# The last stage of a fused transformer kernel put in source order on all compute engines, with the sums of the generated weights moved from GpSimd to VectorE

## The chip, the cores and the metric

The kernel runs on one core of one Trainium2 chip. The metric is the device time of one launch in microseconds, the median of the runs. Lower is better. The engines have short names in the profile: PE is TensorE (PEld its weight loads), DVE is VectorE, ACT is ScalarE, POOL is GpSimd, and SP is SyncE, which here only issues DMAs.

## The reference, cut to what matters

Input `x` has 64 sequences of 64 tokens with 256 features; `cond_256` has a vector of 64 numbers for each sequence. Four layers follow each other, all in float32:

```
x = x + quantised_gelu_ffn(rmsnorm(x) * (cond @ norm_w.T + 1))             # L0
x = x + alpha_a * attention(gamma_a * rmsnorm(x) + beta_a)                 # L1, 16 heads of 16
x = x + alpha_f * (silu(n @ gate_w.T) * (n @ hidden_w.T) @ out_w.T + out_b)
                              # n = gamma_f * rmsnorm(x) + beta_f, 256 -> 1024 -> 256
x = (layernorm(x) * w + b + tanh(cond @ lin_w.T + lin_b)) * w + b          # L2
Wd_b = Wd + 0.1 * (cond @ Wdd.T + bdd)                                     # L3: weights of its own
Wu_b = Wu + 0.1 * (cond @ Wdu.T + bdu)                                     #     for every sequence
x = x + relu(x @ Wd_b.T + bd) @ Wu_b.T + bu                                #     256 -> 128 -> 256
```

## The kernel before

The 4096 tokens are cut into 8 blocks of 512 tokens (`NBLK` = 8, 8 sequences each). Three stages follow each other: L0 (to about 290 us of the profile), attention (to about 470 us), and a last stage with the gated feed-forward layer of L1, the layer norm L2 and the adapter L3. The change is in the last stage and in its opening.

The last stage loops over `n` from 0 to 63; `i, f = divmod(n, 8)` gives the block `i` and the tile `f` of 128 of the 1024 hidden features. The steps of one `n` are:

- `f_products(n)`: 12 matmuls of 512 columns into two banks `gh` (the gate and the hidden value; each float32 product is made of three matmuls of split numbers in `mm3`, lines 83 to 85). There are four `gh` banks.
- `f_inner(n)`: ACT takes silu of the gate (line 622), DVE multiplies it with the value into `sg` (line 623).
- `f_parts(n, sg)`: ACT rounds `sg` to `hhi` (line 642), DVE makes the rest `hlo` (line 643).
- `f_outer(n)`: 12 matmuls of 256 columns that add this tile's share to the two `acc` banks. It is called two steps late, as `f_outer(n - 2)`.

Beside these run, for the block before, its end: `f_residual` (DVE: times alpha, line 667; plus `x2`, line 670; the layer norm's statistics, lines 672 and 673; POOL: the inverse root, lines 182 and 184; DVE: subtract the mean and scale, line 676, called the centring below), `f_weights` (SP loads the generated weights `wd` and `wu` of the block; POOL adds their common part `bias` to them, line 692, four adds of 128x1024 for each block), `f_adapt` (four PE transposes of `x3` and a DVE operation, lines 702 and 703, once for each half `c`), `f_down` and `f_up` (64 small matmuls each, lines 713 and 727). For the block after, `f_start` loads and scales `x2` (lines 191 and 205), and `f_norm` turns it and splits it (lines 212 to 216, 198 and 199). `f_rows` loads two sets of rows, `alpha` and `ab`, and POOL adds `ab` to `x2` (line 606, two adds of 128x512). `f_last` does the end of block 7.

Two ways of ordering are used. Inside `tc.manual_schedule(engines=...)` PE, ACT, DVE and POOL issue in the order of the source; outside it a planner orders each engine's queue by its own costs. Before, the region under manual order opens with attention and closes after `f_outer(3)`, ahead of the loop from `n = 5`. SP is not among its engines: the planner orders the DMAs throughout, and issues a load as soon as its buffer is free. Buffers are counted by tag: `ab` and `alpha` have one each, `wd` and `wu` four, `mm` two banks in this stage.

## Time and profile before

| | |
|---|---|
| median of 3 runs | 807.06 us (805.04 to 807.66) |
| the profiled execution: its own time / span | 804.37 us / 802.2 us |
| PE busy | 763.5 us (95% of the span) |
| DVE, ACT, POOL busy | 567.2, 370.5, 325.7 us |
| PE clock granted, mean | 0.985 |
| chain that ended last | PE 79%, DVE 9%, issue 4%, POOL 3%, DMA 3% |

The page comes from one execution. "Busy" is the time in which an engine works on an instruction. A row of the view by windows gives, for a stretch of time, the busy time of each engine with the number of instructions in parentheses, then the granted PE clock (1.00 is full), the DMA share and GB/s. A row of the timeline gives start, duration, engine, source line, operation, output and inputs with their shapes; a bracket at its end gives the idle time of the engine before it and what ended that.

### The profile page before, as it was taken

How to read it: one execution, taken by the hardware profiler on the slowest of the kernel's cores; microseconds unless marked ns; L12 is line 12 of the kernel's file. 1: busy time of each engine (PE TensorE's matmuls, PEld its weight loads, DVE VectorE, ACT ScalarE, POOL GpSimd, SP SyncE). 2: the span in 40 equal slices, each digit the busy share in tenths (PEclk: the TensorE clock that was granted, in tenths of full speed). 3: DMA queues.
4: the chain of work that ended last, by engine and by line, in shares of the span. 5: the costliest groups of instructions: out<-in, count | busy, mean ns of one | idle time of the engine just before them, and what ended most of it. 6: DMA issues, size and time to landing. Idle time of an engine off the chain costs nothing.

```text
span 802.2 us, 17323 instructions
## 1 busy us (share of the span) xinstructions
PE 763.5 (95%) x7014; PEld 620.2 (77%) x7014; DVE 567.2 (71%) x935; ACT 370.5 (46%) x758; POOL 325.7 (41%) x300
## 2 busy tenths in 40 slices
PE   5999999999999979999999999879999999999996
PEld 3676766667667868888887878778888888888885
DVE  4885866667667679999989875555666666665755
ACT  6524542443443558887877673223233333333130
POOL 2212221222225315545545316945454545454500
PEclk9989999999999999999999999989999999999999
DMA  8997989878884764545655129616161616160401
GB/s 296 308 252 223 233 230 241 203 221 206 190 259 106 145 158 96 131 133 133 153 139 120 40 69 236 131 28 180 35 180 39 173 44 167 50 161 28 133 1 54
DMA packets 117135, 118.87 MB, mean 148 GB/s; under 512 B 39568, under 2 KB 100624, under 8 KB 117056
## 3 DMA queue, kind: packets, MB, share of 16 engines
q1 hardware_dynamic: 109568, 92.40, 46.1%
q0 software_dynamic: 7488, 25.37, 10.4%
q8 instruction: 55, 0.90, 0.5%
q14 instruction: 24, 0.20, 0.1%
HBM read 71.41 MB, written 29.56 MB: 126 GB/s over the span
## 4 chain that ended last, share of the span: by engine, by line
PE 79%; DVE 9%; issue 4%; POOL 3%; DMA 3%; ACT 1%; SPq 0%; DVEq 0%; POOLq 0%; ACTq 0%
PE mm L83 10%; PE mm L84 10%; PE mm L85 10%; PE gh L83 7%; PE gh L85 6%; PE gh L84 6%; PE mm L251 4%; PE acc L85 4%; PE mm L363 4%; PE acc L84 4%; PE acc L83 4%; DMA x2d<-ax 2%; PE mm L520 2%; PE mm L212 2%; PE mm L713 2%
## 5 line engine op out<-in xcount | busy, mean ns | idle before, releaser
L83 PE MATMUL mm<-up,xhl 128*128 128x512 f32 x256 | 108.9, 425 | 2.2 <-ACT up L280 2.2
L84 PE MATMUL mm<-up,xhl 128*128 128x512 f32 x256 | 102.8, 402 | 0.1
L85 PE MATMUL mm<-up,xll 128*128 128x512 f32 x256 | 102.5, 401 | 0.0
L83 PE MATMUL gh<-xhf,gh 128*128 128x512 f32 x244 | 99.2, 407 | 0.0
L84 PE MATMUL gh<-xlf,gh 128*128 128x512 f32 x244 | 95.6, 392 | 0.5 <-POOL xlf L199 0.5
L85 PE MATMUL gh<-xhf,gh 128*128 128x512 f32 x244 | 95.8, 393 | 0.0
L642 ACT CAST hhi<-sg 128x512 fp32r<-128x512 f32 x61 | 37.9, 621 | 119.1 <-DVE sg L623 119.1
L337 DVE SCALAR_TENSOR_TENSOR h<-mm,rs_l,g 128x512 f32<-128x512 f32 x64 | 47.7, 745 | 59.5 <-PE mm L85 36.5
L623 DVE TENSOR_TENSOR sg<-gh,sg 128x512 f32<-128x512 f32 x61 | 41.7, 683 | 64.8 <-PE gh L85 58.2
L85 PE MATMUL acc<-wout,hlo 128*128 128x256 f32 x256 | 74.0, 289 | 7.9 <-DVE hlo L643 7.9
L83 PEld LDWEIGHTS mm<-up,xhl 128*128 128x128 f32 x256 | 49.2, 192 | 38.5 <-issue 18.7
L336 ACT ACTIVATE g<-mm,rs_l 128x512 f32<-128x512 f32 x64 | 44.0, 687 | 73.0 <-PE mm L85 66.9
L83 PE MATMUL acc<-wout,hhi 128*128 128x256 f32 x256 | 73.4, 287 | 1.6 <-ACT hhi L642 1.6
L643 DVE TENSOR_TENSOR hlo<-sg,hhi 128x512 fp32r<-128x512 f32 x61 | 54.6, 895 | 26.7 <-ACT hhi L642 26.3
L84 PE MATMUL acc<-wout,hhi 128*128 128x256 f32 x256 | 73.3, 286 | 0.0
L216 POOL TENSOR_TENSOR xg<-xg,cv 128x512 f32<-128x512 f32 x32 | 33.2, 1046 | 70.7 <-DVE xg L215 70.7
L622 ACT ACTIVATE sg<-gh 128x512 f32<-128x512 f32 x61 | 36.3, 595 | 50.6 <-PE gh L85 50.6
L261 ACT COPY stg<-mm 128x512 f32<-128x512 f32 x64 | 35.3, 587 | 50.9 <-PE mm L251 50.9
L85 PEld LDWEIGHTS mm<-up,xll 128*128 128x128 f32 x256 | 49.0, 192 | 11.9
L84 PEld LDWEIGHTS mm<-up,xhl 128*128 128x128 f32 x256 | 49.3, 193 | 9.8 <-DVE up L281 0.6
L85 PEld LDWEIGHTS acc<-wout,hlo 128*128 128x128 f32 x256 | 49.5, 193 | 8.6 <-DVE hlo L643 8.6
L85 PEld LDWEIGHTS gh<-xhf,gh 128*128 128x128 f32 x244 | 46.0, 188 | 10.7
(189 smaller groups left out, 1905.7 us busy)
## 6 DMA issues: line engine op xcount, KB each, us to landing
gt<-in_g SPq DMA_DIRECT2D x32, 512.0 KB, 4.7
rows<-alphad SPq DMA_DIRECT2D x48, 256.0 KB, 4.0
s1d<-stg POOLq DMA_DIRECT2D x32, 256.0 KB, 5.1
s2d<-stg POOLq DMA_DIRECT2D x32, 256.0 KB, 4.8
vb<-vx SPq DMA_DIRECT2D x32, 256.0 KB, 4.5
wd<-s1d SPq DMA_DIRECT2D x32, 256.0 KB, 4.5
wu<-s2d SPq DMA_DIRECT2D x32, 256.0 KB, 5.6
xf<-in_xT SPq DMA_DIRECT2D x8, 512.0 KB, 7.0
```

What stands on the lines that cost most here:

```text
L83: nc.tensor.matmul(out, lhsT=l[0], rhs=r[0], start=first, stop=False)
L84: nc.tensor.matmul(out, lhsT=l[0], rhs=r[1], start=False, stop=False)
L85: nc.tensor.matmul(out, lhsT=l[1], rhs=r[0], start=False, stop=last)
L216: nc.gpsimd.tensor_tensor(b3(xg), b3(xg), bc(vb, c, i), ALU.add)
L251: nc.tensor.matmul(pb[s][c * 64:(c + 1) * 64], lhsT=gl[h], rhs=gt[h, c * GC:(c + 1) * GC], start=True, stop=True, tile_position=(64 * s, 6 ...
L261: nc.scalar.copy(stg[:, s], pb[s])
L336: nc.scalar.activation(g, pg, AF.Gelu, scale=rs[:, t:t + 1])
L337: nc.vector.scalar_tensor_tensor(h[:, ch * 512:(ch + 1) * 512], pv, rs[:, t:t + 1], g, ALU.mult, ALU.mult)
L622: nc.scalar.activation(sg, pg, AF.Silu)
L623: nc.vector.tensor_tensor(sg, pv, sg, ALU.mult)
L642: nc.scalar.copy(h_hi, sg)
L643: nc.vector.tensor_tensor(h_lo, sg, h_hi.bitcast(F32), ALU.subtract)
```

## The change

1. The manual order now holds to the end of the kernel, so the loop from `n = 5` and `f_last` are issued in source order on PE, ACT, DVE and POOL.
2. The four adds of `bias` go from POOL to DVE (`f_common`) and are spread over the steps `f` = 0, 0, 3 and 6 of the next block.
3. `f_residual` is cut into `f_residual` (`f` = 1), `f_stats` (`f` = 2) and `f_center` (`f` = 3). `f_rows` only loads; the POOL adds of `ab` are `f_base`, called at `f` = 3 of the block's own steps. `f_start` is cut into its load, squares and scaling at `f` = 2, 3 and 4.
4. In the opening, the silu of the three kept tiles is a step of its own (`f_silu`), the first of them inside the last step of attention; `f_inner(4)` and `a_project` change places with products.
5. In the end, the products of tiles 62 and 63 are done for one half of the tokens first, the up products of block 6 come behind them, and `f_last`'s steps are taken by halves. The down products of block 6 go into the loop.

```
 in attention's last step:   todo.append((lambda: None) if tp == 0 else (lambda: f_silu(0)))
...
     s3 = f_inner(3)
     a_weigh(W - 1)
+    f_silu(2)
     s2 = f_kept(2)
     a_parts(W - 1)
     f_outer(0)
+    s4 = f_inner(4)
+    f_parts(2, s2)
     f_outer(1)
-    f_parts(2, s2)
     f_parts(3, s3)
-    a_project(W - 1)
     f_rows(0)
+    f_base(0)
     f_start(1)
-    s4 = f_inner(4)
+    a_project(W - 1)
     f_outer(2)
     f_parts(4, s4)
     f_outer(3)
-    ordered.close()
...
+    for n in range(5, N):
+        i, f = divmod(n, 8)
+        for rest in late:
+            rest()
+        late = []
+        sg = f_inner(n)
+        if i > 0 and f in (4, 5):
+            f_adapt(i - 1, f - 4)
+        if i + 1 < NBLK and f in (5, 6):
+            late = [norm_turn(*fblk[i + 1]["n"], i + 1, f - 5, V_FG, V_FB)]
+        if i > 0 and f == 6:
+            f_down(i - 1)
+        if 0 < i < NBLK - 1 and f == 7:
+            pus = f_up_products(i - 1)
+        f_parts(n, sg)
+        if n > 5:
+            f_outer(n - 2)
+        if 0 < i < NBLK - 1 and f == 7:
+            f_up_store(i - 1, pus)
...
+        if i > 0:
+            if f == 0:
+                f_common(i - 1, "wd", 0)
+                f_common(i - 1, "wd", 1)
+            if f == 1:
+                f_residual(i - 1)
+            if f == 2:
+                f_stats(i - 1)
+            if f == 3:
+                f_center(i - 1)
+                f_base(i)
+                f_common(i - 1, "wu", 0)
+            if f == 6:
+                f_common(i - 1, "wu", 1)
+        if f == 2 and i > 0:
+            f_rows(i)
+            if i + 1 < NBLK:
+                f_load(i + 1)
+        if f == 3 and i + 1 < NBLK and i > 0:
+            f_begin(i + 1)
+        if f == 4 and i + 1 < NBLK and i > 0:
+            f_scale(i + 1)
+        if f == (6 if i + 1 < NBLK else 1):
+            f_weights(i)
...
+    f_last(NBLK - 1)
+    ordered.close()
```

The new helpers, whose bodies were part of `f_rows`, `f_residual` and `f_weights`:

```
+    def f_base(i):
+        x2, ab = fblk[i]["x2"], fblk[i]["ab"]
         for tp in range(TT // 2):
             s = slice(2 * tp, 2 * tp + 2)
             nc.gpsimd.tensor_tensor(x2[:, s], x2[:, s], ab[:, s], ALU.add)
...
+    def f_center(i):
+        B = fblk[i]
+        x3, mv, rs = B["x3"], B["mv"], B["rln"]
         for t in range(TT):
             nc.vector.tensor_scalar(x3[:, t], x3[:, t], mv[:, t, 0:1], rs[:, t:t + 1], ALU.subtract, ALU.mult)
...
+    def f_common(i, which, k):
+        w = fblk[i][which][k]
...
+        nc.vector.tensor_tensor(w, w, row.unsqueeze(1).broadcast_to([P, 4, D]), ALU.add)
```

In `f_last`, the order of the first steps:

```
+        for k in range(2):
+            for n in (8 * i + 6, 8 * i + 7):
+                f_outer(n, range(2 * k, 2 * k + 2))
+        pus = f_up_products(i - 1)
...
+        scaled(0)
+        added(0)
...
+        f_up_store(i - 1, pus)
```

More of the change, by code (lines that the diff above doesn't have):

```diff
@@ L601, in f_rows @@
         fblk[i]["at"] = load_rows(1, "alpha", i)
-        ab = load_rows(2, "ab", i)
-        x2 = fblk[i]["x2"]
+        fblk[i]["ab"] = load_rows(2, "ab", i)
+    def f_base(i):
+        x2, ab = fblk[i]["x2"], fblk[i]["ab"]
         for tp in range(TT // 2):
@@ L630, in f_keep, with f_silu @@
         nc.vector.tensor_copy(room[n][:, 1], pv)
+    def f_silu(n):
+        nc.scalar.activation(room[n][:, 0], room[n][:, 0], AF.Silu)
     def f_kept(n):
         g, v = room[n][:, 0], room[n][:, 1]
-        nc.scalar.activation(g, g, AF.Silu)
         nc.vector.tensor_tensor(g, v, g, ALU.mult)
@@ L644, in f_parts, with f_outer @@
         fun[n] = (h_hi, h_lo)
-    def f_outer(n):
+    def f_outer(n, tiles=range(TT)):
         i, f = divmod(n, 8)
-        h_hi, h_lo = fun.pop(n)
+        h_hi, h_lo = fun[n]
         wout = pools["wout"]
-        if f == 0:
+        if f == 0 and "acc" not in fblk[i]:
             fblk[i]["acc"] = [bank("acc") for _ in range(2)]
         acc = fblk[i]["acc"]
-        for t in range(TT):
+        for t in tiles:
             ts = slice(t * P, (t + 1) * P)
@@ L658, in f_residual, with f_stats @@
     def f_residual(i):
+        B = fblk[i]
+        x3 = B["x3"] = block(f"x3_{i}")
+        for tp in range(TT // 2):
+            s = slice(2 * tp, 2 * tp + 2)
+            nc.vector.tensor_tensor(x3[:, s], B["acc"][tp].rearrange("p (t d) -> p t d", d=D), B["at"][:, s], ALU.mult)
+    def f_stats(i):
         pool = pools["c"]
         B = fblk[i]
-        x2, at = B["x2"], B["at"]
-        x3 = block(f"x3_{i}")
+        x2, x3 = B["x2"], B["x3"]
         st = pool.tile([P, TT, 6], F32, tag="bst", bufs=2, name=f"bst{i}")
-        mv = pool.tile([P, TT, 2], F32, tag="bmv", bufs=2, name=f"bmv{i}")
-        for tp in range(TT // 2):
-            s = slice(2 * tp, 2 * tp + 2)
-            nc.vector.tensor_tensor(x3[:, s], B["acc"][tp].rearrange("p (t d) -> p t d", d=D), at[:, s], ALU.mult)
+        mv = B["mv"] = pool.tile([P, TT, 2], F32, tag="bmv", bufs=2, name=f"bmv{i}")
         for tp in range(TT // 2):
@@ L673, in f_residual @@
                 nc.vector.bn_aggr(mv[:, t], st[:, t])
-        rs = rsqrt(mv[:, :, 1], 1.0, 1e-5, f"ln{i}")
+        B["rln"] = rsqrt(mv[:, :, 1], 1.0, 1e-5, f"ln{i}")
+    def f_center(i):
+        B = fblk[i]
+        x3, mv, rs = B["x3"], B["mv"], B["rln"]
         for t in range(TT):
             nc.vector.tensor_scalar(x3[:, t], x3[:, t], mv[:, t, 0:1], rs[:, t:t + 1], ALU.subtract, ALU.mult)
-        fblk[i] = dict(x3=x3)
     def f_weights(i):
         pool = pools["c"]
-        fblk[i]["wd"], fblk[i]["wu"] = [], []
+        B = fblk[i]
+        B["wd"], B["wu"] = [], []
         for k in range(2):
@@ L689, in f_weights @@
                 nc.sync.dma_start(out=wu[s * 64:(s + 1) * 64], in_=s2d[s, bs].rearrange("b n d -> n b d"))
-            bias = pools["bias"]
-            for w, row in ((wd.rearrange("p b c n -> p b (c n)"), bias[:, 0]), (wu, bias[:, 1])):
-                nc.gpsimd.tensor_tensor(w, w, row.unsqueeze(1).broadcast_to([P, 4, D]), ALU.add)
-            fblk[i]["wd"].append(wd)
-            fblk[i]["wu"].append(wu)
+            B["wd"].append(wd)
+            B["wu"].append(wu)
+    def f_common(i, which, k):
+        w = fblk[i][which][k]
+        if which == "wd":
+            w = w.rearrange("p b c n -> p b (c n)")
+        row = pools["bias"][:, int(which == "wu")]
+        nc.vector.tensor_tensor(w, w, row.unsqueeze(1).broadcast_to([P, 4, D]), ALU.add)
     def f_adapt(i, c):
@@ L716, in f_down, with f_up_products @@
         nc.scalar.activation(B["dn"], pd, AF.Relu, bias=vc[:, 5, 0:1])
-    def f_up(i):
-        B = fblk.pop(i)
-        yo = pools["c"].tile([P, 2, T], F32, tag="yo", bufs=1, name=f"yo{i}")
+    def f_up_products(i):
+        B = fblk[i]
+        pus = []
         for c in range(2):
@@ L728, in f_up, with f_up_store @@
                                      rhs=B["dn"][:, bl], start=True, stop=True, tile_position=(0, 64 * s))
-            nc.vector.scalar_tensor_tensor(yo[:, c], pu, vc[:, 4, c:c + 1], B["x4"][:, c], ALU.add, ALU.add)
+            pus.append(pu)
+        return pus
+    def f_up_store(i, pus):
+        B = fblk.pop(i)
+        yo = pools["c"].tile([P, 2, T], F32, tag="yo", bufs=1, name=f"yo{i}")
+        for c in range(2):
+            nc.vector.scalar_tensor_tensor(yo[:, c], pus[c], vc[:, 4, c:c + 1], B["x4"][:, c], ALU.add, ALU.add)
             nc.sync.dma_start(out=out[c * P:(c + 1) * P, i * T:(i + 1) * T], in_=yo[:, c])
@@ L734, in f_last @@
         pool = pools["c"]
-        B = fblk.pop(i)
+        B = fblk[i]
         x2, at = B["x2"], B["at"]
@@ L741, in f_last, with scaled, added @@
         x4 = pool.tile([P, 2, T], F32, tag="x4", bufs=2, name=f"x4_{i}")
+        dn = pool.tile([P, T], F32, tag="dn", bufs=1, name=f"dn{i}")
+        yo = main.tile([P, 2, T], F32, tag="xn", bufs=1, name=f"yo{i}")
+        sl = [slice(2 * k, 2 * k + 2) for k in range(2)]
+        for k in range(2):
+            for n in (8 * i + 6, 8 * i + 7):
+                f_outer(n, range(2 * k, 2 * k + 2))
+        pus = f_up_products(i - 1)
+        def scaled(k):
+            nc.vector.tensor_tensor(x3[:, sl[k]], B["acc"][k].rearrange("p (t d) -> p t d", d=D), at[:, sl[k]], ALU.mult)
+        def added(k):
+            nc.vector.tensor_tensor(x3[:, sl[k]], x3[:, sl[k]], x2[:, sl[k]], ALU.add)
+        scaled(0)
+        added(0)
         rss = []
         for k in range(2):
-            s = slice(2 * k, 2 * k + 2)
-            nc.vector.tensor_tensor(x3[:, s], B["acc"][k].rearrange("p (t d) -> p t d", d=D), at[:, s], ALU.mult)
-            nc.vector.tensor_tensor(x3[:, s], x3[:, s], x2[:, s], ALU.add)
+            if k == 1:
+                added(1)
             for t in (2 * k, 2 * k + 1):
@@ L749, in f_last @@
                 nc.vector.bn_aggr(mv[:, t], st[:, t])
-            rss.append(rsqrt(mv[:, s, 1], 1.0, 1e-5, f"ln{i}_{k}", 2))
-        f_down(i - 1)
-        f_up(i - 1)
-        dn = pool.tile([P, T], F32, tag="dn", bufs=1, name=f"dn{i}")
-        yo = pool.tile([P, 2, T], F32, tag="yo", bufs=1, name=f"yo{i}")
+            rss.append(rsqrt(mv[:, sl[k], 1], 1.0, 1e-5, f"ln{i}_{k}", 2))
+            if k == 0:
+                scaled(1)
         for k in range(2):
-            hs = slice(k * H, (k + 1) * H)
             for u in range(2):
@@ L759, in f_last @@
                 nc.vector.tensor_scalar(x3[:, t], x3[:, t], mv[:, t, 0:1], rss[k][:, u:u + 1], ALU.subtract, ALU.mult)
+        for k in range(2):
+            hs = slice(k * H, (k + 1) * H)
             pt = bank("gh")
@@ L769, in f_last @@
                     ALU.mult, ALU.add)
+        f_up_store(i - 1, pus)
         for k in range(2):
             hs = slice(k * H, (k + 1) * H)
-            pd = bank("mm")
+            pd = bank("acc")
             for b in range(4):
@@ L780, in f_last @@
             nc.scalar.activation(dn[:, hs], pd[:, :H], AF.Relu, bias=vc[:, 5, 0:1])
-            pu = bank("gh")
-            for b in range(4):
-                bl = slice((4 * k + b) * L, (4 * k + b + 1) * L)
-                for c in range(2):
+        for k in range(2):
+            hs = slice(k * H, (k + 1) * H)
+            for c in range(2):
+                pu = bank("gh")
+                for b in range(4):
+                    bl = slice((4 * k + b) * L, (4 * k + b + 1) * L)
                     for s in range(2):
                         o = c * P + s * 64
-                        nc.tensor.matmul(pu[s * 64:(s + 1) * 64, c * H + b * L:c * H + (b + 1) * L],
+                        nc.tensor.matmul(pu[s * 64:(s + 1) * 64, b * L:(b + 1) * L],
                                          lhsT=B["wu"][k][:, b, o:o + 64], rhs=dn[:, bl],
                                          start=True, stop=True, tile_position=(0, 64 * s))
-            for c in range(2):
-                nc.vector.scalar_tensor_tensor(yo[:, c, hs], pu[:, c * H:(c + 1) * H], vc[:, 4, c:c + 1],
+                nc.vector.scalar_tensor_tensor(yo[:, c, hs], pu[:, :H], vc[:, 4, c:c + 1],
                                                x4[:, c, hs], ALU.add, ALU.add)
@@ L850, in tile_kernel @@
             todo = [lambda: f_keep(0), lambda: f_keep(1)] if tp == 0 else [lambda: f_keep(2), lambda: a_turn(w, 0)]
-            todo.append(lambda: None)
+            todo.append((lambda: None) if tp == 0 else (lambda: f_silu(0)))
         a_score(w)
@@ L904, in tile_kernel @@
     f_parts(0, s0)
+    f_silu(1)
     s1 = f_kept(1)
@@ L911, in tile_kernel @@
     f_outer(0)
+    s4 = f_inner(4)
+    f_parts(2, s2)
     f_outer(1)
-    f_parts(2, s2)
     f_parts(3, s3)
+    f_rows(0)
+    f_base(0)
+    f_start(1)
     a_project(W - 1)
-    f_rows(0)
-    f_start(1)
-    s4 = f_inner(4)
     f_outer(2)
@@ L928, in tile_kernel @@
     bias = pools["bias"] = pools["c"].tile([P, 2, D], F32, name="bias")
-    gbt = main.tile([P, 4, D], F32, tag="xn", bufs=1, name="gbt")
+    gbt = pools["c"].tile([P, 4, D], F32, tag="yo", bufs=1, name="gbt")
     nc.sync.dma_start(out=gbt, in_=gb)
-    for k in range(2):
-        nc.vector.scalar_tensor_tensor(bias[:, k], gbt[:, 2 * k + 1], 0.1, gbt[:, 2 * k], ALU.mult, ALU.add)
-    for n in range(5, N + 2):
+    late = []
+    for n in range(5, N):
         i, f = divmod(n, 8)
-        if n < N:
-            f_parts(n, f_inner(n))
-        if n == N:
-            f_weights(NBLK - 1)
+        for rest in late:
+            rest()
+        late = []
+        sg = f_inner(n)
[8 more added lines that the diff above has]
+        f_parts(n, sg)
@@ L939, in tile_kernel @@
         if n > 5:
             f_outer(n - 2)
-        if f == 1 and 0 < i < NBLK:
-            f_residual(i - 1)
-            f_weights(i - 1)
-        if i == NBLK:
-            continue
-        if f == 3:
+        if 0 < i < NBLK - 1 and f == 7:
+            f_up_store(i - 1, pus)
+        if n == 7:
+            for k in range(2):
+                nc.vector.scalar_tensor_tensor(bias[:, k], gbt[:, 2 * k + 1], 0.1, gbt[:, 2 * k], ALU.mult, ALU.add)
+        if i > 0:
[12 more added lines that the diff above has]
+                f_common(i - 1, "wu", 1)
@@ L947, in tile_kernel @@
+        if f == 2 and i > 0:
             f_rows(i)
             if i + 1 < NBLK:
-                f_start(i + 1)
-        if i + 1 < NBLK and f in (5, 6):
-            f_norm(i + 1, f - 5)
-        if i > 0:
-            if f in (4, 5):
-                f_adapt(i - 1, f - 4)
-            if f == 6 and i + 1 < NBLK:
-                f_down(i - 1)
-            if f == 7 and i + 1 < NBLK:
-                f_up(i - 1)
+                f_load(i + 1)
+        if f == 3 and i + 1 < NBLK and i > 0:
+            f_begin(i + 1)
@@ L959, in tile_kernel @@
+        if f == 4 and i + 1 < NBLK and i > 0:
+            f_scale(i + 1)
+        if f == (6 if i + 1 < NBLK else 1):
+            f_weights(i)
+        for which, k in {N - 4: (("wd", 0), ("wd", 1)), N - 3: (("wu", 0),), N - 2: (("wu", 1),)}.get(n, ()):
+            f_common(NBLK - 1, which, k)
     f_last(NBLK - 1)
+    ordered.close()
 def kernel(x, cond_256, L0_cond_norm_w, L0_cond_up_w, L0_cond_down_w, L1_cond_attn_gamma_w,
```

## The prediction

> **What bounds the kernel now.** I read the page first, for the engine that sets the time. The rows of 40 slices (20 us each) show PE near full everywhere, with dips in the last stage at slices 24 and 27, and at the end.

> ```profile
> PE   5999999999999979999999999879999999999996
> PEclk9989999999999999999999999989999999999999
> ```

> The view by windows puts numbers on the stage. Its columns are the busy times of PE, PEld, DVE, ACT and POOL, the granted PE clock, the DMA share and GB/s.

> ```profile
> 460.00:480.00 20.00, 18.09 (x163) 15.63 (x164) 15.98 (x23) 13.88 (x25) 2.58 (x2) 0.91 0.32 87
> 520.00:540.00 20.00, 14.30 (x110) 13.06 (x112) 11.84 (x21) 4.69 (x8) 10.08 (x9) 0.83 0.10 27
> 580.00:600.00 20.00, 20.00 (x189) 17.69 (x184) 10.97 (x13) 7.28 (x17) 12.38 (x6) 1.00 0.61 166
> 600.00:620.00 20.00, 20.00 (x166) 17.82 (x165) 14.53 (x31) 5.71 (x10) 7.90 (x8) 1.00 0.19 47
> 780.00:802.00 22.00, 15.25 (x295) 13.83 (x293) 11.11 (x28) 2.26 (x4) 1.85 (x4) 0.92 0.14 49
> ```

> From 540 to 780 us PE has no gap at all at full clock. There nothing can be won, only lost. What can be won are three places: the opening, 518 to 530 us, and the end. The timeline shows the first two.

> ```profile
> 472.81 0.39 PE L83 MATMUL acc<-wout,hhi 128*128 128x256 f32 x1 [1.64 <-ACT hhi L642]
> 469.46 1.28 ACT L634 ACT_TABLE_LOAD   x1
> 525.70 0.58 PE L85 MATMUL acc<-wout,hlo 128*128 128x256 f32 x1 [7.67 <-DVE hlo L643]
> 519.91 2.34 POOL L692 TENSOR_TENSOR wu<-wu,bias 128x1024 f32<-128x1024 f32 x1
> 522.61 1.02 POOL L184 TENSOR_TENSOR rs_ln<-ms_ln,nhalf 128x4 f32<-128x4 f32 x1
> 523.66 1.38 DVE L676 TENSOR_SCALAR x<-x,bmv,rs_ln 128x256 f32<-128x256 f32 x4 [9.70 <-POOL rs_ln L184]
> ```

> In the opening PE waits for the first `hhi`, which waits for ACT's table load and silu. At 518 PE waits for `hlo`, behind the centring (L676) on DVE, which waits for the inverse root on POOL, which stands behind eight adds of the common part.

> **What is won.** Opening: PE has done its last transposes at 471.17 and starts `f_products(5)` at 485.08. Between lie four `f_outer` at 1.44 us (12 matmuls, 0.12 apart), `a_project` 1.44 and `f_products(4)` 2.80 (12 at 0.233): 10.0 us. With the table load and the first silu in ACT's idle time after 465.5, the first `hlo` is ready at about 471.3, and the next waits fall behind the moved `f_products(4)`. PE would be at `f_products(5)` at 481.2: 3.9 us, of which 1.9 is idle time and the rest mostly half clock (windows of 0.7 us show 0.50 from 474.9 to 477.7).

> Middle: the four adds leave POOL, so the 7.67 us go, and what the half clock adds after them: ten products 0.21 instead of 0.12 apart (0.9), four transposes 0.71 instead of 0.44, the next two products 0.91 instead of 0.47: 1.6. Together 9.3. A wait of 0.5 at 498 for `xlf`, which now has more than a step of room, goes too.

> End: from the last issue of `f_products(63)`, at 779.17, to the end of the span are 23.0 us, with the down products of block 6 (2.0) in them. These now come before. Afterwards, counted from there: half 0 of the accumulators at 3.1 (waiting for `hlo`), scaled and added 4.5, statistics 5.7, root 6.7, while half 1 goes through DVE to 8.1 and its root to 9.1; centring to 9.9; turned halves 10.7 and 11.5; down products at the lowered clock that they ran at before (about 2 us for the first half), relu 0.45, up products, last output operation at 16.8, and 2.7 from there to the end as before: 19.5. With the 2.0: 21.5, a gain of 1.5 (between a loss of 1 and a gain of 3.5, as the clock falls).

> Sum: 3.9 + 9.3 + 0.5 + 1.5 = 15.2 us.

> **What the moved adds cost.** An operation of 1024 elements on DVE takes 1.22 us (rows L490, L492), 1.14 apart: 4.6 us for a block. DVE is busy 25.5 of 40 us in a block (the two rows above), so there is room. By steps: one `f` is 4.24 us of PE; DVE needs from `sg` to the end of `hlo` 1.99. At `f` = 0 two adds make it 4.3, at `f` = 1 the residual's two operations 3.2: the accumulators are free 0.7 us before PE wants them. At `f` = 6 the add ends about 0.7 us before the up products reach it. Zero, covered by PE's own 4 us; if that cover were 1 us short, 7 us over seven blocks. The loads of `wd` and `wu` are issued a block ahead by SP, which stays with the planner.

> **What the order costs: steps 2 to 4.** DVE may now take nothing before its turn. Let 0 be the moment at which PE has issued the products of `f` = 2. PE issues those of `f` = 4 by 8.48 and then at once the four transposes of `f_adapt`, which need the centred `x3`, done by 8.92. DVE starts `sg` at 0.27 and ends `hlo` at 2.26 (rows: `sg` at 590.24, `hlo` at 591.62, next free 0.61 later). `f_stats` follows: two adds 0.69, four statistics 0.39, four aggregations; a dependent operation starts 0.04 after the end of the one ahead (L490 at 461.95 for 1.22, L492 at 463.20), so 2 x 0.73 + 4 x 0.43 + 4 x 0.08 = 3.5. The next `sg` starts at 5.76, its `hlo` at 7.14, and centring's four at 7.75, 0.33 apart, the last ending at 9.2. So even alone DVE is 0.4 us late for PE.

> But it is not alone. The root (0.08 + 0.28 + 1.02 after the last aggregation at 5.84) is done at 7.2, and next on POOL stand the two adds of `f_base`, which wait for nothing else: `ab` has its buffer since the last block, and before the change SP issued these rows as soon as the buffer came free. They meet `hlo` and the centring. What such a meeting does is seen here (two places, DVE and POOL):

> ```profile
> 507.77 2.30 DVE L670 TENSOR_TENSOR x<-x,fx 128x512 f32<-128x512 f32 x1
> 509.49 1.74 POOL L606 TENSOR_TENSOR fx<-fx,rows 128x512 f32<-128x512 f32 x1
> 510.00 1.78 DVE L670 TENSOR_TENSOR x<-x,fx 128x512 f32<-128x512 f32 x1
> 511.19 1.74 POOL L606 TENSOR_TENSOR fx<-fx,rows 128x512 f32<-128x512 f32 x1
> 568.08 0.34 DVE L205 TENSOR_SCALAR xnf<-fx,rs_f 128x256 f32<-128x256 f32 x1
> 568.24 1.32 POOL L606 TENSOR_TENSOR fx<-fx,rows 128x512 f32<-128x512 f32 x1 [2.09 <-DVE xnf L205]
> 568.34 1.37 DVE L205 TENSOR_SCALAR xnf<-fx,rs_f 128x256 f32<-128x256 f32 x1
> ```

> The same operation takes 0.68 us alone. Here each engine stands while the other works, and they take turns; the scaling of `x2` (L205), 0.34 alone, stood 1.03 longer behind a POOL add. Centring (L676) has the same form, but all its 28 take 0.40 to 0.41: the trace never shows it beside a wide POOL add. Bounds: no meeting, 0.4 us late; taking turns, 7.14 + 0.61 + 2 x 1.30 + 4 x 0.33 + 0.1 = 11.8 and PE 2.9 us late. I take 2.9, by L205, its nearest row. It happens in blocks 1 to 7: 7 x 2.9 = 20.3 us. After that DVE has caught up by `f` = 5.

> [...]

> Then the clock. Idle time of 1.9 us between 471.2 and 473.5 was followed by half clock for 3.3 us, which costs 1.7; gaps of 1.1 to 1.4 in attention were not. So a stall of 2.9 costs between 0 and 1.7 more; I take half of the seven: 6.0.

> [...]

> **Sum.** 802.2 - 15.2 + 20.3 + 6.0 = 813.3 us of span. The profiled execution took 804.37, and the median of the runs is 807.06, 4.9 above the span: 818.

> **Rivals.** First, the cheap meeting: POOL's adds come late (rows not yet there) or centring does not stand behind them. Then 807.06 - 15.2 + 7 x 0.4 = 794.7, faster; without the tail's gain 796, and with a better clock there 793. For it: no L676 ever ran beside POOL. Against: L205. It decides as soon as DVE is under about 1.5 us late at `f` = 4.

> Second, a half meeting, one POOL add in the way: 1.6 us a block, under the length that cost clock: 807.06 - 15.2 + 11.2 = 803, from 800 to 806.

> Third, a new wait on the loads: DVE now stands for `wd`, and behind it `sg` and `hlo`, so PE. In the old profile these adds waited up to 5.2 us for `wu`. If the planner issues the loads only at their place in the source, 2 us in seven blocks on top of the forecast: 832. Against it: `wd` of block 0 was loaded at 459, 35 us early.

> **How the numbers follow.** Forecast (POOL and DVE take turns) 0.60, with its own range 809 to 824 (from a stall of 2.4 without loss of clock to 2.9 with 1.7, in seven blocks); cheap meeting 0.27; half meeting 0.08; loads 0.05. 0.3%, about 2.4 us, is what a measurement can tell. Slower: 0.60 + 0.05. Faster: 0.27 and half of the half meeting, 0.31; the rest, 0.04, the same. The forecast's case alone does not hold 8 in 10, so the range reaches down to the cheap meeting: 793 to 826.

> **What would show it.** In the profile after: no POOL row L692; PE without gaps from 469 to about 525; then, once in each block, idle PE at the transposes of `f_adapt` with the centring as releaser, POOL's two adds of `ab` in the same microseconds, centring rows of 1.3 us and more, and a granted clock of 0.50 behind some of them. If centring rows stay at 0.4 and PE at 20.00 of 20, the forecast is wrong and the time is near 795. A PE gap at `f` = 1 or 7 instead would mean the adds on DVE cost what I put at zero.

## The result and the profile after

The changed kernel takes 817.92 us (median of 4 runs, 817.19 to 819.53) against 806.94 us (805.04 to 807.66, 4 runs) before: a ratio of 1.0146 (95% interval 1.0123 to 1.0169). It is slower by 11.0 us, against 11 forecast. The profiled execution took 818.64 us with a span of 816.8 us and a mean granted clock of 0.979. Its span is 14.6 us longer than that of before; 2.7 us of that were there at `n` = 3, before the change counts: the half clock at the boundary of the first two stages (293 us) lasted 6.83 us in this execution and 3.41 in the other, and the same code of attention ran some 2 us longer at full clock. All ten traces of this document have this code ahead of `n` = 3 (but for the place of one silu), and reach `n` = 3 between 462.6 and 471.5 us; a few microseconds between two medians are therefore read in the traces, from `n` = 3 on.

The page's rows of 40 slices: the dips of PE at slices 26 and 27 are gone, and so is the long half clock.

```profile
PE   6999999999999979999999999999999999999997
PEclk9989999999999989999999999999999999999999
```

The loss is too thin for these digits. The view by windows shows it (PE, PEld, DVE, ACT, POOL busy, clock, DMA share, GB/s):

```profile
460.00:480.00 20.00, 19.43 (x290) 16.44 (x290) 16.82 (x20) 13.25 (x22) 7.74 (x6) 1.00 0.40 110
520.00:540.00 20.00, 20.00 (x225) 17.60 (x224) 12.78 (x20) 5.90 (x10) 5.05 (x4) 1.00 0.33 95
560.00:580.00 20.00, 19.06 (x162) 16.20 (x163) 12.69 (x20) 5.50 (x10) 7.07 (x7) 0.91 0.30 79
600.00:620.00 20.00, 18.45 (x149) 15.31 (x149) 12.86 (x22) 6.65 (x17) 9.16 (x9) 0.91 0.11 31
800.00:816.80 16.80, 10.92 (x214) 9.63 (x212) 10.99 (x26) 0.95 (x2) 1.90 (x4) 0.90 0.18 63
```

The opening and the middle are nearly full now. But the stretch at 600 us, which had 20.00 of 20 at clock 1.00, has 18.45 at 0.91. The view of waits for PE in the last stage names one cause in the blocks (first row) and one at the end:

```profile
PE mm L720 <- DVE x L688: 10.8, 14, 0.9
PE gh L801 <- DVE x L795: 2.7, 2, 2.2
```

(us in total, times, longest; L720 are the transposes of `f_adapt`, L688 is the centring, L676 before; L801 and L795 are the same two steps in `f_last`.) The timeline of one block shows the meeting:

```profile
601.71 0.69 DVE L647 TENSOR_TENSOR hlo<-sg,hhi 128x512 fp32r<-128x512 f32 x1 [0.69 <-ACT hhi L646]
601.78 1.75 POOL L608 TENSOR_TENSOR fx<-fx,rows 128x512 f32<-128x512 f32 x1
602.31 1.37 DVE L688 TENSOR_SCALAR x<-x,bmv,rs_ln 128x256 f32<-128x256 f32 x1
603.49 1.31 POOL L608 TENSOR_TENSOR fx<-fx,rows 128x512 f32<-128x512 f32 x1
603.61 1.35 DVE L688 TENSOR_SCALAR x<-x,bmv,rs_ln 128x256 f32<-128x256 f32 x1
604.88 0.72 DVE L688 TENSOR_SCALAR x<-x,bmv,rs_ln 128x256 f32<-128x256 f32 x2
603.74 0.33 PE L720 MATMUL mm<-ident,x 128*128 128x128 f32 x1 [0.61 <-DVE x L688]
605.01 0.97 PE L720 MATMUL mm<-ident,x 128*128 128x128 f32 x3 [0.94 <-DVE x L688]
```

The first centring, 0.40 alone, ends 0.15 us after POOL's first add; POOL's second add then runs, and the second centring ends 0.16 after it; the last two, with POOL gone, need 0.72 together. PE idles 0.61 before the first transpose and 0.94 before the second: the four take 2.77 us in place of 0.44. The same two gaps, to 0.01 us, stand in all seven blocks (517, 560, 604, 648, 690, 734 and 778 us). Behind five of the seven the clock fell to half (0.50) for 3.41 us; the first row below is a block where it did, the second one where it did not:

```profile
562.30:565.80 3.50, 3.50 (x15) 3.11 (x14) 3.47 (x8) 0.62 (x1) 0.00 (x0) 0.52 0.60 148
650.00:653.50 3.50, 3.50 (x22) 3.10 (x21) 3.47 (x8) 1.23 (x2) 0.17 (x1) 1.00 0.55 150
```

**Where the time went.** The start of `f_products(n)` in the two timelines gives the account. In the blocks, from tile 6 of one to tile 6 of the next (before: 39.74 us, in the last one 39.29):

| stretch | before | after | difference | half clock behind the stall |
|---|---|---|---|---|
| up to `n` = 3 | 466.54 | 469.22 | +2.7 | (code that is the same) |
| `n` 3 to 5, opening | 18.54 | 15.43 | -3.1 | |
| `n` 5 to 12 | 29.75 | 29.08 | -0.7 | |
| `n` 12 to 14 | 19.30 | 12.21 | -7.1 | no |
| `n` 14 to 22, 22 to 30 | 39.74 each | 43.97, 43.98 | +8.5 | yes, yes |
| `n` 30 to 38 | 39.74 | 42.46 | +2.7 | no |
| `n` 38 to 46, 46 to 54 | 39.74 each | 43.96, 43.94 | +8.4 | yes, yes |
| `n` 54 to 62 | 39.29 | 43.54 | +4.25 | yes |
| `n` = 62 to the end | 30.10 | 29.06 | -1.0 | |

Two tiles with neither stall took 9.63 in the other blocks of before. So the row of `n` 12 to 14 is a gain of 9.7 and a first loss of 2.6. Gains: 3.1 + 0.7 + 9.7 + 1.0 = 14.5 us (15.2 forecast). Losses: 2.6 + 8.5 + 2.7 + 8.4 + 4.25 = 26.4 us (26.3 forecast).

### The profile page after: what moved, and what is told of

Same layout as the page of the kernel before. It is cut to its first block, busy times and chain, and to the rows that moved or that the text cites. A ratio compares the mean times of both kernels' runs of the same rounds, so it can differ in the third digit from the quotient of the medians.

```text
span 816.8 us, 17303 instructions
## 1 busy us (share of the span) xinstructions
PE 776.5 (95%) x7014; PEld 623.4 (76%) x7014; DVE 601.7 (74%) x967; ACT 371.4 (45%) x758; POOL 247.0 (30%) x268
## 4 chain that ended last, share of the span: by engine, by line
PE 77%; DVE 15%; issue 3%; ACT 2%; DMA 1%; POOL 1%; SPq 0%; POOLq 0%; DVEq 0%
PE mm L83 11%; PE mm L84 10%; PE mm L85 10%; PE gh L83 5%; PE gh L84 5%; PE gh L85 5%; PE mm L251 4%; PE mm L363 4%; PE acc L83 3%; PE acc L85 3%; PE acc L84 3%; PE mm L520 2%; DVE x L688 2%; PE mm L731 2%; PE mm L212 2%
## 5 line engine op out<-in xcount | busy, mean ns | idle before, releaser
L83 PE MATMUL mm<-up,xhl 128*128 128x512 f32 x256 | 108.5, 424 | 2.2 <-ACT up L280 2.2
L85 PE MATMUL mm<-up,xll 128*128 128x512 f32 x256 | 102.2, 399 | 0.0
L83 PE MATMUL gh<-xhf,gh 128*128 128x512 f32 x244 | 99.1, 406 | 0.0
L84 PE MATMUL gh<-xlf,gh 128*128 128x512 f32 x244 | 98.4, 403 | 0.0
L85 PE MATMUL gh<-xhf,gh 128*128 128x512 f32 x244 | 97.9, 401 | 0.0
L83 PEld LDWEIGHTS mm<-up,xhl 128*128 128x128 f32 x256 | 49.0, 191 | 38.4 <-issue 19.5
L83 PE MATMUL acc<-wout,hhi 128*128 128x256 f32 x256 | 76.7, 300 | 0.0
L85 PE MATMUL acc<-wout,hlo 128*128 128x256 f32 x256 | 74.4, 291 | 0.5 <-DVE hlo L647 0.5
L647 DVE TENSOR_TENSOR hlo<-sg,hhi 128x512 fp32r<-128x512 f32 x61 | 44.2, 724 | 41.2 <-ACT hhi L646 40.8
L84 PE MATMUL acc<-wout,hhi 128*128 128x256 f32 x256 | 73.9, 289 | 0.0
L216 POOL TENSOR_TENSOR xg<-xg,cv 128x512 f32<-128x512 f32 x32 | 35.4, 1115 | 77.5 <-DVE xg L215 77.5
L85 PEld LDWEIGHTS mm<-up,xll 128*128 128x128 f32 x256 | 48.9, 191 | 11.8
L85 PEld LDWEIGHTS gh<-xhf,gh 128*128 128x128 f32 x244 | 47.1, 193 | 11.2
L182 POOL TENSOR_SCALAR ms_ln<-bmv 128x4 f32<-128x4 f32 (+1 forms) x9 | 1.8, 201 | 175.9 <-DVE bmv L681 150.5
```

The lines of the kernel that those rows point to most:

```text
L83: nc.tensor.matmul(out, lhsT=l[0], rhs=r[0], start=first, stop=False)
L84: nc.tensor.matmul(out, lhsT=l[0], rhs=r[1], start=False, stop=False)
L85: nc.tensor.matmul(out, lhsT=l[1], rhs=r[0], start=False, stop=last)
L216: nc.gpsimd.tensor_tensor(b3(xg), b3(xg), bc(vb, c, i), ALU.add)
L647: nc.vector.tensor_tensor(h_lo, sg, h_hi.bitcast(F32), ALU.subtract)
```

## The experiments

The theory: POOL's adds of `ab` (`f_base`), now at `f` = 3, and the centring on DVE take turns; PE stands at the transposes of `f_adapt`, and the clock falls behind some of the stalls. Rivals: DVE, in the order of the source, is late for `f_adapt` by itself; or the four adds on DVE cost it. The times are medians, the ratios are to the kernel before on the same chips. Kernel 1 is that of experiment 1, and so on; kernel 3 is also called version 3.

**1. `f_base` at `f` = 0** (with its load of `ab` beside it), the rest as changed:

```
             if f == 0:
                 f_common(i - 1, "wd", 0)
                 f_common(i - 1, "wd", 1)
+                f_base(i)
...
-                f_base(i)                    # at f == 3
```

> The changed kernel, with POOL's two adds of ab (f_base) called at f = 0 and not at f = 3, so that they are done before the inverse root of the layer norm. Theory (POOL and DVE take turns at the centring): the four centring rows fall from about 0.4, 1.3 and 1.3 us to 0.4 each, the wait of PE at the transposes of f_adapt falls from 2.3 to about 0.4 us a block, and no half clock follows it: 25.9 us of loss become 2.8, so 818 becomes about 795. Rival (DVE's queue in source order is too late by itself, POOL does not matter): PE still waits about 2 us a block, the time stays within 3 us of 818.

Measured: 797.06 us (795.73 to 798.5), ratio 0.9897 (0.9857 to 0.9938). The whole loss is gone and 8 us are won. The line's durations (min, median, max in ns), first of the changed kernel, then of this one:

```profile
L688 DVE TENSOR_SCALAR x<-x,bmv,rs_ln x28: 399/876/1373, 515.9 to 779.5; 128x256 f32<-128x256 f32 x28
```

```profile
L688 DVE TENSOR_SCALAR x<-x,bmv,rs_ln x28: 404/407/409, 516.1 to 760.3; 128x256 f32<-128x256 f32 x28
  PEld mm L720: 3.9, 21
```

No centring is slowed, and PE has 20.00 of 20 at clock 1.00 at 600 us:

```profile
600.00:620.00 20.00, 20.00 (x222) 17.52 (x221) 12.74 (x19) 5.90 (x10) 9.36 (x7) 1.00 0.24 70
```

What is left is the last line of the view above: PE's weight loads wait 3.9 us in all for the centring. A block (`n` 14 to 22) takes 40.55, 0.8 more than before, of which 0.3 is this (version 3 below, without the wait, takes 40.25); that DVE alone is about 0.4 us late was forecast. The order and the adds did not make the loss: its cause is the place of `f_base`.

**2. The other way round: `f_base` stays, PE gets other work first.** `f_adapt(i - 1, 0)` goes behind `f_outer(n - 2)` at `f` = 4:

```
-        if i > 0 and f in (4, 5):
-            f_adapt(i - 1, f - 4)
+        if i > 0 and f == 5:
+            f_adapt(i - 1, 1)
...
             f_outer(n - 2)
+        if i > 0 and f == 4:
+            f_adapt(i - 1, 0)
```

> The changed kernel, with the 12 products of f_outer ahead of the transposes of f_adapt at f = 4, so that PE has 1.44 us of work in the place of the wait; POOL's adds stay where they are. Theory: the wait falls from 2.3 to 0.9 us a block, in pieces of under 1 us, and granted clock stays at 1.00: 7 x 0.9 = 6.3 us of loss in the place of 25.9, about 798. Rival on the clock (any wait costs half clock, however short): 1.7 us more in five of seven blocks, about 807. Rival on the wait (something else holds PE): no change, 818.

Measured: 805.84 us (801.32 to 807.11), ratio 0.9994 (0.9966 to 1.0022): the size of the gain was missed. POOL and DVE meet as before, and the stall shrank as expected, but a new wait stands behind it:

```profile
PE mm L212 <- DVE xnf L205: 3.6, 6, 0.6
PE mm L720 <- DVE x L688: 2.5, 7, 0.4
```

The meeting still makes DVE late: its four centrings take 3.33 us at 599.2, against 1.38 in version 3 below. `f_adapt` now also stands behind `f_parts` in the source, so its DVE operation (L721) comes behind `hlo`: it starts at 605.56, while its transposes have been done since 602.9. The scaling of `x2` for the next block (L205) stands behind it on DVE, and the transposes of `f_norm` (L212), at `f` = 5, wait for that. Against version 3, slot `f` = 4 takes 1.0 and slot `f` = 5 0.9 us longer in a block. The clock stays at 1.00 through the blocks: thirteen single gaps of 0.35 to 0.61 us never lowered it here.

**3. Both edits.**

> The changed kernel with both edits: POOL's adds at f = 0 and f_outer ahead of the transposes at f = 4. Theory: PE has no gap in the seven blocks, all of the 25.9 us come back and what was won at the opening, the middle and the end stays: about 792. Rival (moved adds of the common part cost VectorE time that shows once the other waits are gone): a gap of about 1 us a block at f = 2 or f = 7, about 799.

Measured: 792.52 us (790.24 to 797.55), ratio 0.9849 (0.9802 to 0.9896). PE has no gap in seven blocks, and the view of waits between the opening and the end is empty for it. A whole block in one window reads:

```profile
584.00:624.00 40.00, 40.00 (x337) 34.90 (x336) 27.30 (x47) 12.94 (x28) 11.79 (x10) 1.00 0.42 106
```

The second edit won 12.1 us alone and 4.5 between the medians on top of the first, where the intervals of the two ratios overlap; in the profiled executions, from `n` = 3 to the end, it is 3.0 (325.9 and 322.9). Without the collision DVE is early enough for `f_norm`. This version beats both kernels, and experiments 5 to 8 start from it.

**4. The kernel before with the sums on DVE alone** (one word of line 692, order by the planner):

```
-                nc.gpsimd.tensor_tensor(w, w, ...)
+                nc.vector.tensor_tensor(w, w, ...)
```

> The kernel before with one edit: the four adds of the common part on VectorE in the place of GpSimd, everything else and the planner's order unchanged. Theory: the 7.67 us gap at 518 us and the half clock behind it go, as the inverse root no longer stands behind these adds; the rest of the stage stays without gaps: about 797.5. Rival (the adds now stand in VectorE's queue ahead of hlo and wait for their loads): the gap moves to VectorE and the time is 803 to 807.

Measured: 797.56 us (791.33 to 798.97), ratio 0.9888 (0.9837 to 0.9939). The middle's 7.67 us are gone; one gap of 1.46 is left there:

```profile
522.25 0.66 PE L702 MATMUL mm<-ident,x 128*128 128x128 f32 x4 [1.46 <-DVE x L703]
```

From `n` = 12 to 14 it takes 11.43 us against 19.30. So 7.9 of the 9.7 us won here come from the adds' change of engine; the order of the source is needed for the last 1.8 at most. From `n` = 3 to the end the profiled executions take 335.7 us before, 347.6 changed, 327.0 here and 322.9 in version 3: this one word wins 8.7, the order with its places put right 4.1 more, and the order as it was first placed lost 20.6 against the word alone.

**5. Version 3 with the sums back on POOL** (`f_common` on GpSimd).

> e3_both with the four adds of the common part back on POOL, at the same places of the source. Theory (POOL and DVE take turns, and the adds on DVE cost nothing): the add of wu at f = 3 now stands on POOL right behind the inverse root, as f_base did, and meets the centring with one operation of about 2.4 us: DVE ends the centring 2.4 us later, PE waits about 1.2 us a block at f_adapt with f_outer ahead of it, 7 x 1.2 = 8 us, so about 801. Rival (the adds on DVE were a cost of their own): DVE is freed of 4.6 us a block, the time falls to about 790 or stays at 792.5.

Measured: 807.92 us (806.49 to 812.5), ratio 1.0037 (1.0013 to 1.0061): 15.4 us slower than version 3, where about 9 had been expected. The turns are seen again, with longer adds. In blocks 1 to 6 one add of `wu` meets the centring, which costs 1.0 us a block. At 765 us, where the adds for the last block follow each other on POOL, all four centrings are caught:

```profile
764.88 2.88 POOL L712 TENSOR_TENSOR wu<-wu,bias 128x1024 f32<-128x1024 f32 x1
765.40 2.50 DVE L688 TENSOR_SCALAR x<-x,bmv,rs_ln 128x256 f32<-128x256 f32 x1
767.71 2.39 POOL L712 TENSOR_TENSOR wd<-wd,bias 128x1024 f32<-128x1024 f32 x1
772.40 2.38 POOL L712 TENSOR_TENSOR wu<-wu,bias 128x1024 f32<-128x1024 f32 x1
772.51 2.42 DVE L688 TENSOR_SCALAR x<-x,bmv,rs_ln 128x256 f32<-128x256 f32 x1
770.30 0.33 PE L720 MATMUL mm<-ident,x 128*128 128x128 f32 x1 [2.02 <-DVE x L688]
```

Each centring ends 0.1 to 0.2 us after the POOL add that it stands behind. PE waits three times about 2 us there, and half clock follows from 771 to 777 us (mean 0.76 from 764 to 778). From `n` = 5 to 63 the kernel took 300.61 us against 286.34; with 5.8 in six blocks, this one place costs 8.4, and the expectation had no term for it.

**6. Version 3 with the old opening** (silu, `f_inner(4)`, `f_parts(2)`, `a_project` where they were).

> e3_both with the opening in the old order (first silu after attention's last step, a_project before the loads, f_inner(4) after them). Theory (the new opening is worth what the trace shows between the third and the fifth products, 3.1 us, by PE's wait for the first hhi and the half clock behind it): about 795.5, with a PE gap of about 1.6 us at f_outer(0). Rival (opening worth nothing, as its gap is made good later by queues that run ahead): 792.5.

Measured: 797.72 us (796.8 to 798.14), ratio 0.9909 (0.9873 to 0.9945), 5.2 slower than version 3. The old wait is back:

```profile
473.66 0.39 PE L83 MATMUL acc<-wout,hhi 128*128 128x256 f32 x1 [1.65 <-ACT hhi L646]
```

From `n` = 3 to 5 it needs 18.48 us against 15.43: the opening is worth 3.05, as expected. The rest is not the opening's: in the profiled executions (mean clock 0.984, and 0.994 in version 3) 2.4 us more are spent after `n` = 61, with half clock from 784 to 791 us over code that is the same and had none in version 3.

**7. Version 3 with tiles 62 and 63 whole in the accumulators.**

```
-        for k in range(2):
-            for n in (8 * i + 6, 8 * i + 7):
-                f_outer(n, range(2 * k, 2 * k + 2))
+        for n in (8 * i + 6, 8 * i + 7):
+            f_outer(n)
```

> e3_both with the products of tiles 62 and 63 for all tokens one after the other, not by halves. Theory (half 0 of the accumulators ends 0.72 us earlier by halves, and the chain of the end starts from it): 0.7 us longer, about 793.2, hardly more than can be measured; the trace shows the first operation on the accumulators 0.7 us later after the last products. Rival (the halves are all of the end's 1.5 us): 794 or more.

Measured: 794.31 us (787.3 to 798.51), ratio 0.9859 (0.9817 to 0.9901). The runs scatter over 11 us, so the time alone decides nothing. In the trace the first operation on the accumulators (L774 here, L775 there) starts 17.74 us after `f_products(61)`, against 17.13: the halves are worth 0.6 us on this path. After `n` = 61 this execution takes 1.6 us more than version 3's; it has half clock from 785 to 788 us, which the other has not (mean clock 0.987 and 0.994), and that this is the other 1.0 fits but was not tried.

**8. Version 3 with `f_base(0)` behind `a_project`**, away from the opening's `keep` and `hlo`.

> e3_both with POOL's two adds for block 0 in the opening called behind a_project and not ahead of it. Theory (they met the first two multiplications and the first hlo on DVE, which took 1.20, 0.99 and 1.76 us in place of 0.69): these rows fall to about 0.69, PE starts its fifth products about 0.5 to 0.9 us earlier, about 791.8. Rival (ACT sets the opening): the rows fall, PE starts at the same time, 792.5.

Measured: 791.95 us (791.15 to 797.56), ratio 0.9855 (0.9816 to 0.9893): the same as version 3 (792.52). The time is as expected, but not by the expected way. The opening gains 0.3 (15.13 against 15.43). Then POOL is late with `xlf`, which stands behind the moved adds:

```profile
493.51 0.51 PE L84 MATMUL gh<-xlf,gh 128*128 128x512 f32 x1 [0.54 <-POOL xlf L199]
```

From `n` = 5 to 63 it loses 1.3. The collision was moved, not saved.

## Why the prediction was right, step by step

The mechanism is the one forecast: POOL's adds of `ab` and the centring take turns, PE stands at `f_adapt`, the clock falls behind some of the stalls. Experiment 1 shows that it is this meeting (21 us, from 818 to 797, hang on it, with the place of two adds and their load as the only edit); experiment 5 shows it again with other adds. That the total fits to 0.1 us has luck in it: several terms were off and cancelled. Two readings were off as well and carried little: the digits of the page dip at slices 26 and 27, while slice 24 reads 9, so that the opening shows in the window of 460 to 480 us alone; and 9.2 against 8.92 makes DVE alone 0.3 us late, which the stall of 2.9 goes by, not the 0.4 of the cheap meeting.

- **The stall** was put at 2.9 us a block and is 2.33: 16.3 in place of 20.3. The mis-sized term is the two POOL adds at 1.30 each on DVE's path. The first add began 0.07 us after `hlo` and stood behind it, so part of it had passed before centring was due: the first two centrings lost 0.97 + 0.95 = 1.9, not 2.6. The last ended 11.1 us after PE's products of `f` = 2, against 11.8.
- **The clock** was put at half of seven stalls, 1.7 each, 6.0. It fell behind five; a block with it took 43.96 and one without it 42.46, so 1.5 each, 7.5 in all.
- **Not priced at all**: PE's rhythm. 42.46 - 39.74 - 2.33 leaves 0.4 us a block, some 2.6 in seven. Here and in version 3 an undisturbed step of PE takes 4.24 us, in blocks 1 to 7 of before and of kernel 4 4.19. It is told below, and its cause is open.
- **The opening** was put at 3.9 and gained 3.1. The step that failed was the readiness of the first `hlo`, worked out as if DVE were alone. With the silu earlier, `keep` meets POOL's add of attention (L572); and `f_base(0)`, which the change also moves forward and which was counted as nothing, meets `hlo` and the next `keep` (0.69 each alone). Rows of the changed kernel:

```profile
471.25 1.29 POOL L572 TENSOR_TENSOR ax<-ax,ax 128x512 f32<-128x512 f32 x1 [4.15 <-DVE ax L571]
471.34 0.63 DVE L522 COPY pts<-mm 128x512 f32<-128x512 f32 x1
471.89 1.20 DVE L639 TENSOR_TENSOR keep<-keep 128x512 f32<-128x512 f32 x1
472.49 3.41 POOL L608 TENSOR_TENSOR fx<-fx,rows 128x512 f32<-128x512 f32 x2
473.77 1.00 DVE L647 TENSOR_TENSOR hlo<-keep,hhi 128x512 fp32r<-128x512 f32 x1 [0.69 <-ACT hhi L646]
474.69 1.77 DVE L639 TENSOR_TENSOR keep<-keep 128x512 f32<-128x512 f32 x1
```

  In kernel 8 `hlo` and the second `keep` are 0.69 again and the first `keep` is still 1.20: 0.3 us of the missing 0.8 is `f_base(0)`'s; that the other 0.5 is the first meeting's fits its length but was not tried.
- **The middle** was put at 9.3 and gained 9.7; the wait for `xlf` 0.5 and 0.7. Kernel 4 shows that 7.9 of it needed only the adds on DVE.
- **The adds on DVE** were put at zero: there is no gap of PE at `f` = 1 or 7, and version 3, which has them, fills PE.
- **The end** was put at 1.5 (-1 to 3.5) and gained 1.0, with half clock in it from 808 to 811 us, as the kernel before has it from 792 to 796; at full clock, in version 3, the same code took 27.5 us from `n` = 62, a gain of 2.6. The bound was right to be wide.
- **The rivals.** Cheap meeting: the kernel of experiment 1 is what it described, at 797 where 794.7 was worked out; the rhythm (0.4 in seven blocks) is the size of the difference. It failed since POOL was free and the rows of `ab` were there: its first add begins as the inverse root (L184) ends, at 601.8, without a wait for a transfer. Half meeting: no, both adds met the centring. Loads: no add of L712 waited for a transfer.

## What to carry to other kernels

When work is put in a fixed order, list for each engine what it is now free to do while another engine runs the operation that the bottleneck waits for; two adds on an idle engine, in the wrong microsecond, cost 21 us over seven blocks here, and three steps earlier nothing. In the rows of the changed kernel and of experiment 5 a centring that met a POOL add ended 0.1 to 0.2 us after that add: 0.40 alone, it took 1.37 beside an add of 1.75 and 2.50 beside one of 2.88. An estimate from these rows prices such a meeting at up to one POOL operation for each DVE operation that stands behind one. Not every operation stood: the copy L522 (`pts<-mm`) took 0.63 us beside POOL's add at 471.25, no more than its other rows (0.63 to 0.68). And an edit that moves work off the path (experiment 2) should be followed one step on: who stands behind it on the same engine, and who waits for that.

## What the runs showed of the hardware

```profile
L84 PEld LDWEIGHTS acc<-wout,hhi x160: 187/189/192, 562.8 to 758.4; 128*128 128x128 f32 x160
```

```profile
L84 PEld LDWEIGHTS acc<-wout,hhi x159: 187/192/192, 559.9 to 759.8; 128*128 128x128 f32 x159
```

  In kernel 4 a step takes 4.19 us behind a gap of 0.35 at 494.57, 4.24 behind one of 0.40 at 505.48, and 4.19 again from 540 us on. In kernel 6 the rhythm changes at 498.9 us in the middle of the products, without a gap. In kernels 1 and 2 every such step takes 4.24 us from 497 us to the last block. What sets it stays open; no run here tried it. At 0.05 us in each of some 60 steps it is worth an estimated 3 us of the stage, which version 3 does not have.
